# Attention layers of four batches in one sequence, with the projection row broadcast through DRAM

## The chip, the cores and the metric

The kernel runs on one core of one Trainium2 chip. The metric is the device time of one execution in microseconds (us). Three runs of the kernel before took 3220.69, 3226.43 and 3228.97 us; their median, 3226.43 us, is the time before.

## What is computed

Four layers of a graph network act on `x`, 16 batches of 1024 nodes with 256 features, all in float32. `adj` is a 1024 x 1024 matrix with few nonzero entries. Layers 0 and 1 make messages along the edges. Layers 2 and 3, which the change is about, are two attention layers of the same form:

```python
feats  = einsum('bni,oi->bno', data, W1)
f1     = einsum('bno,o->bn', feats, W2) + b2[0]
logits = f1[:, :, None] + f1[:, None, :]
coefs  = softmax(leaky_relu(logits) + adj, axis=-1)
vals   = einsum('bij,bjo->bio', coefs, feats)
out    = vals + bias2 + data
```

Each logit is a sum of a number of the row's node and a number of the column's node. So the kernel needs f1 twice: as a column, one number on each partition for each tile of 128 nodes, and as a row, the same 1024 numbers on every partition.

## The kernel before

The 16 batches are worked on in four groups of four (`GB = 4`). `z` holds a batch's features, feature-major, in two halves of 128 features. A tile of nodes has 128 of them, so a batch has `NT = 8` tiles; a half `v` of the nodes has `HN = 512`, which is `HT = 4` tiles.

A group has these stages. `with_edges` ends layer 0: it loads scores (`gd`, 512 KB each) and multiplies them with `hw` of all four batches. `layer_one` is layer 1, of two batches at a time: `projected`, and then `neighbours`, whose 16 steps load each 256 KB of the turned adjacency matrix (`adjT_in`, L1122, a ring of three buffers) and multiply. `pair_layers` holds the attention layers of the same two batches. In groups 0 to 2 a group is `with_edges`, `layer_one` of batches 0 and 1, their `pair_layers`, `layer_one` of batches 2 and 3, their `pair_layers`. The last group has work of its own beside it (`far_ahead`).

An attention layer of one batch is one `front` and two `sums`. `front` (L969) projects: eight tiles of two products each, 128x257 out, where column 257 is f1; ScalarE copies each tile from PSUM to `feats` (L980). Then come the `scales` (L988): eight TensorE transposes (L1002), each of a column of f1 stretched to 128 x 128 by an access pattern of step zero, so that its transpose is f1 as a row on all partitions; one more transpose (L1007) for the largest f1; VectorE's reduction of that (L1008); two ScalarE instructions that evict the rows with a Relu (L1011); exponentials (L1014 to L1016); eight scalings of `feats` (L1018). `sums` (L1027) makes for each of the eight tiles `jt` a weight tile `m` of 128 x 512 on VectorE (L1036, four buffers), multiplies it on TensorE into four PSUM banks, and hands the sums to `finish`. For layer 2 that is `second`, which divides by the totals (L1049, L1210) and transposes back (L1217, L1221); for layer 3 `third`, which adds the residual (L1241, L1247, L1251) and stores from ScalarE's queue (L1252).

Most TensorE products go through one helper, so their line is L126; they are told apart by the tiles that they read. One product has two records.

`scales` and the transposes back are not written where they are made but put on a list, `later`, which `catch_up` empties at the second tile of the next `front` or the first tile of the next `sums`. The order of a pair is written out by hand:

```python
                m0 = yield from front(z[0], gat2)
                m1 = yield from front(z[1], gat2)
                yield from sums(m0, 0, second(0))
                yield from sums(m0, 1, second(0))
                yield from sums(m1, 0, second(1))
                m0 = yield from front(z[0], gat3)
                yield from sums(m1, 1, second(1))
                yield from sums(m0, 0, third(0))
                m1 = yield from front(z[1], gat3)
                ahead()
```

and three more `sums`. `ahead` loads for the next group four `hw` (L892, 1024 KB each, from a pool of five buffers that `feats` and `y` use too) and four `z` (L900, 1024 KB each, into the four buffers of the present `z`).

Beside all this runs a side stream, the edge scores of the next groups. One step of it is a gather on GpSimd's queue (L695), two VectorE passes over 128 x 1024 (L805 and L807) and four ScalarE sums (L811), later a scatter (L700). `Side.along` writes such steps between the steps of the main work, 0.255 of a step per microsecond that a main step is said to take (the numbers in `yield`). `paced` makes the first pass of a step wait for a product six back, so that a side step does not run far ahead of the main work. The framework that writes the queues keeps near the order of the program text, but may put a later instruction first where an earlier one is not ready.

Of the kernel before, what the change touches and what calls it, by code (L numbers as in the profile page):

```python
# [9 lines left out]
F32 = mybir.dt.float32  # L10
# [55 lines left out]
def gnn_stack_kernel(  # L66
# [120 lines left out]
    class Attention:  # L187


        def __init__(self, W1, W2, b2, bias2, name):  # L190
            self.W1 = W1
            self.w2 = column(W2, f"{name}_w2")
            self.b2 = everywhere(b2, 1, f"{name}_b2")
            self.bias2 = column(bias2, f"{name}_bias2c")
            self.wT = const.tile([P, DH, D + 1], F32, name=f"{name}_wT")
            self.rows = const.tile([P, DH, P], F32, name=f"{name}_rows")

        def prepare(self, nat):
            transpose_weight(self.wT[:, :, :D], nat)
            ps = bank()  # L200
            for dh in range(DH):
                for oh in range(DH):
                    nc.tensor.matmul(
                        ps[:, dh : dh + 1], nat[:, oh, dh * P : (dh + 1) * P], self.w2[:, oh : oh + 1],
                        start=oh == 0, stop=oh == DH - 1,
                    )
            nc.vector.tensor_copy(self.wT[:, :, D], ps[:, :DH])
            for dh in range(DH):
                nc.vector.tensor_copy(self.rows[:, dh, :], self.wT[:, dh, D : D + 1].to_broadcast([P, P]))
# [26 lines left out]
    def prepare(t):  # L236
        transpose_weight(l1wT, t[:, 0])
        for i, gat in enumerate((gat2, gat3)):
            gat.prepare(t[:, 1 + i])
# [22 lines left out]
    part_d = dram.tile([XT * P + P, 2 * D], F32, name="part_d")  # L262

# [411 lines left out]
    with tc.If(listed > 0) as arm:  # L675
        with ExitStack() as stack:
# [292 lines left out]
            def front(x, weights):  # L969

                wT = weights.wT
                f = ttile("feats").rearrange("p (t d) -> p t d", t=NT)
                for jt in range(NT):
                    ps = bank()
                    for dh in range(DH):
                        product(
                            ps[:, : D + 1], x[:, dh, jt * P : (jt + 1) * P], wT[:, dh, :],
                            start=dh == 0, stop=dh == DH - 1,
                        )
                    nc.scalar.activation(f[:, jt, :], ps[:, : D + 1], AF.Copy)  # L980
                    if jt == 1:
                        catch_up()
                    yield 0.86
                made = {}
                later.append(lambda: scales(f, weights, made))
                return made

            def scales(f, weights, made):  # L988
# [4 lines left out]
                ta = small.tile([P, NT], F32, tag="tau", name="tau")  # L993
# [16 lines left out]
                for v in range(NV):  # L1010
                    nc.scalar.activation(r[:, v * HN : (v + 1) * HN], banks[v], AF.Relu, bias=sh[:, 3:4])  # L1011
                nc.vector.tensor_scalar(sh[:, 1:2], sh[:, 0:1], -0.01, None, ALU.mult)
# [8 lines left out]
            later = []  # L1021

            def catch_up():
                while later:
                    later.pop(0)()

            def sums(made, v, finish):  # L1027

                if "f" not in made:
                    catch_up()  # L1030
# [3 lines left out]
                for jt in range(NT):  # L1034
# [9 lines left out]
                    if jt == 0:  # L1044
                        catch_up()
# [71 lines left out]
            def neighbours(y, z, cols):  # L1117
                n = cols.stop - cols.start
                acc = [[bank() for _ in range(DH)] for _ in range(2)]
                for jt in range(NT):  # L1120
                    a = three.tile([P, HN], F32, tag="a", name="adjT_in")[:, :n]
                    nc.sync.dma_start(a, adjT_d[jt][:, cols])  # L1122
                    for i in range(2):
                        for eh in range(DH):
# [3 lines left out]
                            )  # L1128
                    yield 3.4 * n / HN
# [66 lines left out]
            def pair_layers(b, z, ahead, first):  # L1196


                yield from first


                def second(i):
                    def finish(v, acc, share):
                        cols = slice(v * HN, (v + 1) * HN)
                        vals = []
                        for c in range(HT):
                            if c % 2 == 0:
                                pair = four.tile([P, 2, D], F32, tag="st", name="val")
                            val = pair[:, c % 2, :]
                            nc.scalar.activation(val, acc[c][:, :D], AF.Identity, scale=share[:, c : c + 1])  # L1210
                            vals.append(val)

                        def turn_back():
                            ps = [bank() for _ in range(DH)]
                            for c in range(HT):
                                for dh in range(DH):
                                    nc.tensor.transpose(  # L1217
                                        ps[dh][:, c * P : (c + 1) * P], vals[c][:, dh * P : (dh + 1) * P], ident
                                    )
                            for dh in range(DH):  # L1220
                                nc.vector.scalar_tensor_tensor(  # L1221
                                    z[i][:, dh, cols], ps[dh], gat2.bias2[:, dh : dh + 1], z[i][:, dh, cols],
                                    ALU.add, ALU.add,
                                )
                        later.append(turn_back)
                    return finish


                def third(i):
                    def finish(v, acc, share):  # L1230
                        if v == 0:
                            for dh in range(DH):
                                nc.scalar.activation(
                                    z[i][:, dh, :], z[i][:, dh, :], AF.Identity, bias=gat3.bias2[:, dh : dh + 1]
                                )
                        for c in range(0, HT, 2):
                            ps = bank()
                            it = v * HT + c
                            for k in range(2):
                                for dh in range(DH):  # L1240
                                    nc.tensor.transpose(  # L1241
                                        ps[:, k * D + dh * P : k * D + (dh + 1) * P],
                                        z[i][:, dh, (it + k) * P : (it + k + 1) * P], ident,
                                    )
                            st = four.tile([P, 2, D], F32, tag="st", name="st")
                            for k in range(2):
                                nc.scalar.activation(  # L1247
                                    st[:, k, :], acc[c + k][:, :D], AF.Identity, scale=share[:, c + k : c + k + 1]
                                )
                            both = st.rearrange("p t d -> p (t d)")  # L1250
                            nc.vector.tensor_tensor(both, both, ps, ALU.add)  # L1251
                            nc.scalar.dma_start(  # L1252
                                out[b + i, it * P : (it + 2) * P].rearrange("(t p) d -> p t d", p=P), st
                            )
                    return finish


                m0 = yield from front(z[0], gat2)
                m1 = yield from front(z[1], gat2)
                yield from sums(m0, 0, second(0))  # L1260
                yield from sums(m0, 1, second(0))
                yield from sums(m1, 0, second(1))
                m0 = yield from front(z[0], gat3)
                yield from sums(m1, 1, second(1))
                yield from sums(m0, 0, third(0))
                m1 = yield from front(z[1], gat3)
                ahead()
                yield from sums(m0, 1, third(0))
                yield from sums(m1, 0, third(1))
                yield from sums(m1, 1, third(1))  # L1270
                assert not later

            def ahead(g):
                if g < NGR:
                    loaded.append(([load_hw(g * GB + i) for i in range(GB)], load_z(g)))
                    for load, i in z_loads:
                        load(i)
                    z_loads.clear()
# [22 lines left out]
            for g in range(NGR):  # L1301
# [4 lines left out]
                one = pair_layers(g * GB, z[:2], lambda: None, layer_one(z[:2]))  # L1306
                if g < NGR - 1:
                    side.along(one, RATE[1])
                    side.along(pair_layers(g * GB + 2, z[2:], lambda: ahead(g + 1), layer_one(z[2:])), RATE[1])
                else:  # L1310
                    for _ in far_ahead(z[2:], one):
                        pass
                    for _ in pair_layers(g * GB + 2, z[2:], lambda: None, from_lists(z[2:], msg)):
                        pass
# [3 lines left out]
    with arm.Else():  # L1318
        with ExitStack() as stack:
# [15 lines left out]
            prepare(load_naturals(stage))  # L1335
# [110 lines left out]
```

## Time and profile before

| What | Value |
|---|---|
| Median of three runs | 3226.43 us |
| The profiled execution's own time | 3225.44 us |
| Its span, first to last instruction | 3224.0 us |
| TensorE busy | 3128.0 us, 97% |
| VectorE busy | 2353.0 us, 73% |
| ScalarE busy | 1946.6 us, 60% |
| GpSimd busy | 1816.5 us, 56% |
| Mean granted TensorE clock | 0.99 |
| Moved by DMA | 687.48 MB, 213 GB/s |

The rows of the profile show one execution. PE is TensorE's matmuls, PEld its weight loads, DVE is VectorE, ACT is ScalarE, POOL is GpSimd and SP is SyncE; a `q` behind the name is the engine's queue of instructions, where DMAs are issued. In a group of instructions the numbers are the busy time, the mean duration of one in ns, and the idle time of the engine before them with what ended it. Durations of neighbouring instructions overlap, since they are pipelined: what one costs is the distance from start to start.

### The profile page before, as it was taken

To read this page: it belongs to the slowest core of one execution; us is meant where nothing else is said; L and a number is where in the kernel's file an instruction comes from. 1 tells how busy PE (TensorE), PEld (TensorE's weight loads), DVE (VectorE), ACT (ScalarE), POOL (GpSimd) and SP (SyncE) were. 2 spreads that over 40 slices of the span, in tenths; PEclk is the share of its full clock that TensorE was granted. 3 is DMA by queue.
4 is the path that set the end of the run, shared out by engine and by line. 5 is a ranking of instruction groups with operands and counts; after the bars stand their busy time and mean duration, and the time that the engine had idled before them with its cause. 6 is when DMAs were issued, how large, how long until landed. Compare 5 with 4: busy or idle time off the path is not lost. (4 is left out here: it accounts for less than half of the span.)

```text
span 3224.0 us, 39221 instructions
## 1 busy us (share of the span) xinstructions
PE 3128.0 (97%) x12122; PEld 2205.5 (68%) x12122; DVE 2353.0 (73%) x3174; ACT 1946.6 (60%) x6512; POOL 1816.5 (56%) x1483
## 2 busy tenths in 40 slices
PE   9899999999999999999999999899999999999899
PEld 5444545555457668678876867787687688858787
DVE  7797778677774689789768978877798891148744
ACT  3244555666668777567977757688676774414242
POOL 1146777676764666657566665556676651076600
PEclk9999999999999999999999999999999999999999
DMA  9888888888889765756876575587657644475600
GB/s 321 294 320 317 266 288 270 273 239 247 269 280 343 207 172 148 230 156 206 293 235 170 158 219 178 164 285 236 188 151 213 186 141 144 126 251 147 172 3 28
DMA packets 281898, 687.48 MB, mean 213 GB/s; under 512 B 45184, under 2 KB 137344, under 8 KB 274512
## 3 DMA queue, kind: packets, MB, share of 16 engines
q0 software_dynamic: 128224, 387.80, 41.3%
q1 hardware_dynamic: 126016, 245.98, 22.2%
q10 hardware_dynamic: 27440, 51.13, 4.2%
q8 instruction: 97, 1.59, 0.2%
q14 instruction: 121, 0.99, 0.1%
HBM read 553.45 MB, written 131.32 MB: 212 GB/s over the span
## 5 line engine op out<-in xcount | busy, mean ns | idle before, releaser
L811 ACT ACTIVATE z<-z 128x256 f32<-128x256 f32 x2432 | 979.5, 406 | 639.1 <-DVE z L807 580.9
L805 DVE TENSOR_TENSOR z<-z,u 128x1024 f32<-128x1024 f32 x608 | 738.7, 1220 | 437.0 <-PE bank L126 274.6
L126 PE MATMUL bank<-feats,m 128*128 128x257 f32 x4096 | 921.3, 383 | 19.3 <-DVE m L1036 17.8
L695 POOL DMA_INDIRECT z<-v_d,slot_v x512 | 637.2, 1244 | 479.9 <-ACT z L811 274.3
L126 PEld LDWEIGHTS bank<-feats,m 128*128 128x128 f32 x4096 | 770.6, 191 | 137.9 <-DVE m L1036 20.0
L700 POOL DMA_INDIRECT dense_d<-gt,slot_at x512 | 645.9, 1262 | 186.5 <-issue 140.1
L807 DVE SCALAR_TENSOR_TENSOR z<-z,w2r 128x1024 f32<-128x1024 f32 x608 | 737.9, 1220 | 9.0
L126 PE MATMUL bank<-gc,hw 128*128 128x256 f32 x2048 | 458.9, 386 | 25.2 <-ACT gc L1064 15.5
L811 ACT ACTIVATION_READ_ACCUMULATOR z<-z 128x1 f32 x2432 | 461.6, 190 | 0.0
L126 PEld LDWEIGHTS bank<-gc,hw 128*128 128x128 f32 x2048 | 390.6, 193 | 93.1 <-ACT gc L1064 24.0
L126 PE MATMUL bank<-adj_sb,h 128*128 128x512 f32 x1024 | 444.6, 594 | 4.5 <-ACT st L322 3.0
L1036 DVE SCALAR_TENSOR_TENSOR m<-rho,tau,adj_sb 128x512 f32<-128x512 f32 x512 | 375.3, 743 | 67.8 <-PE bank L126 62.1
L126 PE MATMUL bank<-adjT_in,y 128*128 128x512 f32 (+1 forms) x960 | 401.0, 579 | 2.0 <-DMA adjT_in<-adjT_d 1.4
L126 PEld LDWEIGHTS bank<-adj_sb,h 128*128 128x128 f32 x1024 | 194.9, 191 | 245.5 <-issue 239.8
L126 PE MATMUL bank<-w,hT 128*128 128x512 f32 (+1 forms) x1024 | 336.3, 489 | 0.0
L126 PEld LDWEIGHTS bank<-adjT_in,y 128*128 128x128 f32 x960 | 181.9, 190 | 216.8 <-issue 204.2
L1064 ACT ACTIVATE gc<-gd 128x1024 f32<-128x1024 f32 x128 | 264.7, 2071 | 95.3 <-PE bank L126 60.8
L126 PEld LDWEIGHTS bank<-w,hT 128*128 128x128 f32 x1024 | 195.7, 192 | 142.4 <-issue 122.9
L126 PE MATMUL bank<-g_wT,z 128*128 128x257 f32 x1024 | 234.0, 383 | 2.5 <-DVE z L1115 2.5
L695 POOL DMA_INDIRECT z<-v_d,x_node x96 | 122.2, 1273 | 176.2 <-ACT z L811 118.7
L126 PEld LDWEIGHTS bank<-g_wT,z 128*128 128x128 f32 x1024 | 193.2, 192 | 33.4 <-DVE z L1115 3.5
L695 POOL DMA_INDIRECT z<-y_d,slot_v x96 | 108.3, 1128 | 56.6 <-DVE msg L1174 41.0
(161 smaller groups left out, 2370.2 us busy)
## 6 DMA issues: line engine op xcount, KB each, us to landing
gd<-dense_d SPq DMA_DIRECT2D x128, 512.0 KB
dense_d<-zero ACTq DMA_DIRECT2D x64, 512.0 KB
adjT_in<-adjT_d SPq DMA_DIRECT2D x112, 256.0 KB
h<-in_x_dram SPq DMA_DIRECT2D x19, 1024.0 KB
u_d<-st SPq DMA_DIRECT2D x64, 256.0 KB
v_d<-st SPq DMA_DIRECT2D x64, 256.0 KB
hw_d<-st SPq DMA_DIRECT2D x64, 256.0 KB
u<-u_d POOLq DMA_DIRECT2D x32, 512.0 KB
```

The lines of the kernel that those rows point to most:

```text
L126: recent.append(nc.tensor.matmul(*args, **kw))
L695: return nc.gpsimd.indirect_dma_start(out=dst, out_offset=None, in_=src[:], in_offset=bass.IndirectOffsetOnAxis(ap=at, axis=0), **how,)
L700: return nc.gpsimd.indirect_dma_start(out=dst[:], out_offset=bass.IndirectOffsetOnAxis(ap=at, axis=0), in_=src, in_offset=None,)
L805: paced(nc.vector.tensor_tensor(z, z, u, ALU.add))
L807: nc.vector.scalar_tensor_tensor(zk, zk, 0.0, w2r[:, None, :].to_broadcast([P, GB, D]), ALU.max, ALU.mult)
L811: nc.scalar.activation(zk[:, c, :], zk[:, c, :], AF.Copy, accum_out=s[:, k, c : c + 1])
L1036: nc.vector.scalar_tensor_tensor(m, r[:, cols], ta[:, jt : jt + 1], ea[:, jt, cols], ALU.max, ALU.mult)
L1064: paced(nc.scalar.activation(gc, gd.rearrange("p n i -> p i n"), AF.Copy), 16)
```

## The change

In groups 0 to 2 the two `pair_layers` become one `group_layers`: `layer_one` of batches 0 and 1, the projection of batch 0, `layer_one` of batches 2 and 3, and then a sequence over eight pairs (layer, batch), in which the projection of the next pair is written before the sums of the present one. The loads for the next group are written at the last two of the eight. `scales` is kept for the last group. In the others `to_row` and `from_row` take its place: VectorE gathers f1 as a 128 x 9 tile (eight columns and the maximum of each partition), TensorE transposes it once, ScalarE copies the 9 x 128 result, SyncE stores it to a row in DRAM and loads that row back to all 128 partitions (512 KB, and 64 KB for the maxima). Three ticks later VectorE reduces the maxima and one ScalarE Relu of 128 x 1024 works on the loaded row. `later` now holds counts, and `tick`, called at every second tile of `sums`, every fourth of `front` and every step of `neighbours`, counts them down. The list `rows` that a fallback branch uses is moved into that branch.

```diff
+            def tick():
+                for what in later:
+                    what[0] -= 1
+                while later and later[0][0] <= 0:
+                    later.pop(0)[1]()
...
-            def front(x, weights):
+            def front(x, weights, row=None):
...
-                    if jt == 1:
-                        catch_up()
+                    if jt % 4 == 1:
+                        tick()
                     yield 0.86
                 made = {}
-                later.append(lambda: scales(f, weights, made))
+                if row is None:
+                    later.append([1, lambda: scales(f, weights, made)])
+                else:
+                    later.append([1, lambda: to_row(f, weights, made, row)])
                 return made
+
+            def to_row(f, weights, made, row):
+
+                r = two.tile([P, N], F32, tag="rho", name="rho")
+                tops = two.tile([P, P], F32, tag="tops", name="tops")
+                column = small.tile([P, NT + 1], F32, tag="column", name="column")
+                nc.vector.tensor_copy(column[:, :NT], f[:, :, D])
+                nc.vector.tensor_reduce(column[:, NT:], f[:, :, D], AX.X, ALU.max)
+                ps = bank()
+                nc.tensor.transpose(ps[: NT + 1, :P], column, ident)
+                nc.scalar.activation(r[: NT + 1, :P], ps[: NT + 1, :P], AF.Copy)
+                nc.sync.dma_start(row.rearrange("(t p) -> t p", p=P), r[: NT + 1, :P])
+                nc.sync.dma_start(r, bcast_rows(row[:N], N))
+                nc.sync.dma_start(tops, bcast_rows(row[N:], P))
+                later.append([3, lambda: from_row(f, weights, made, r, tops)])
+
+            def from_row(f, weights, made, r, tops):
+                sh = small.tile([P, 4], F32, tag="shift", name="shift")
+                nc.vector.tensor_reduce(sh[:, 0:1], tops, AX.X, ALU.max)
+                nc.vector.scalar_tensor_tensor(sh[:, 3:4], weights.b2, 2.0, sh[:, 0:1], ALU.mult, ALU.add)
+                nc.scalar.activation(r, r, AF.Relu, bias=sh[:, 3:4])
+                scaled(f, made, r, sh)
...
             def sums(made, v, finish):
 
-                if "f" not in made:
-                    catch_up()
+                while "f" not in made:
+                    tick()
...
-                    if jt == 0:
-                        catch_up()
+                    if jt % 2 == 0:
+                        tick()
                     yield 1.7
...
+            def group_layers(g, z):
...
+                def fronts(layer, i):
+                    gat = (gat2, gat3)[layer]
+                    made[layer, i] = yield from front(z[i], gat, row_d[layer, g * GB + i])
...
+                yield from layer_one(z[:2])
+                yield from fronts(0, 0)
+                yield from layer_one(z[2:])
+                order = [(layer, i) for layer in range(2) for i in range(GB)]
+                for n, it in enumerate(order):
+                    if n + 1 < len(order):
+                        yield from fronts(*order[n + 1])
+                    if n == 2 * GB - 2:
+                        hw = [load_hw((g + 1) * GB + i) for i in range(GB - 1)]
+                        nz = load_z(g + 1)
+                    if n == 2 * GB - 1:
+                        hw.append(load_hw((g + 1) * GB + GB - 1))
+                        loaded.append((hw, nz))
+                    for _ in range((0, 2, 1)[max(0, n - 2 * GB + 3)]):
+                        load, i = z_loads.pop(0)
+                        load(i)
+                    yield from both_halves(*it)
...
-                one = pair_layers(g * GB, z[:2], lambda: None, layer_one(z[:2]))
                 if g < NGR - 1:
-                    side.along(one, RATE[1])
-                    side.along(pair_layers(g * GB + 2, z[2:], lambda: ahead(g + 1), layer_one(z[2:])), RATE[1])
+                    side.along(group_layers(g, z), RATE[1])
```

`scaled` is the rest of `scales` from L1012 on, unchanged; `both_halves` is the two `sums` of one pair with their `finish`; `second` and `third` take `z` as an argument and put the transposes back on `later` with a count of 1.

## The prediction, made before the changed kernel was run

> **What bounds the kernel now.** I read the page first, then windows cut at the stages, then the chain of waits and the timelines of one pair of batches.
>
> ```profile
> PE 3128.0 (97%) x12122; PEld 2205.5 (68%) x12122; DVE 2353.0 (73%) x3174; ACT 1946.6 (60%) x6512; POOL 1816.5 (56%) x1483
> ```
>
> TensorE has work 97% of the span, so whatever leaves TensorE can shorten the kernel, unless another engine is full in that stage. The windows tell (PE, PEld, DVE, ACT, POOL busy; granted clock; DMA share; GB/s): two pairs of attention layers and the layer one between the first and the second.
>
> ```profile
> 1156.00:1311.00 155.00, 152.04 (x740) 130.59 (x739) 144.61 (x216) 113.20 (x421) 102.93 (x77) 1.00 0.56 158
> 1311.00:1380.00 69.00, 69.00 (x196) 36.77 (x195) 48.42 (x49) 40.97 (x166) 44.61 (x36) 1.00 0.73 221
> 1726.00:1881.00 155.00, 152.01 (x736) 129.27 (x735) 145.51 (x216) 114.07 (x422) 104.32 (x81) 1.00 0.57 161
> ```
>
> In the attention stage VectorE is busy 145 of 155 us, in layer one only 48 of 69. The 73% of the page is a mean over both. The clock is 1.00: nothing is lost there. Next, pieces of the chain (start, length):
>
> ```profile
> 2968.61 0.87 PE bank L1002 x8
> 2969.48 0.11 PE bank L1007
> 2969.59 13.88 PE bank L126 x64
> ```
>
> Eight stretched transposes hold TensorE 0.87 us, one 0.11 us, and half of a batch's sums (64 records) 13.88 us, 0.217 us a record. A pair of batches is then 4 projections of 32 records (27.8), 8 halves (111.0), 4 x 0.98 of row transposes and 8 x 0.87 of other transposes (7.0): 149.7 us, against 155 measured. The waits of TensorE over the three groups:
>
> ```profile
> PE bank L126 <- DVE m L1036: 17.8, 9, 8.1
> PE bank L126 <- issue: 4.5, 4, 2.5
> ```
>
> VectorE's weight tile `m` is what TensorE waits for. Two of the nine are 11.4 us together, and there VectorE itself sat for a gather of the side stream:
>
> ```profile
> 2046.41 1.23 DVE L805 TENSOR_TENSOR z<-z,u 128x1024 f32<-128x1024 f32 x1 [8.19 <-DMA z<-v_d,slot_v]
> ```
>
> The remaining 6.4 us are the change's to win; one is the start of a pair, where the scaled `feats` come late:
>
> ```profile
> 1173.17 2.84 PE L126 MATMUL bank<-feats,m 128*128 128x257 f32 x12 [1.99 <-DVE m L1036]
> ```
>
> **The change part by part.** Times are set against the profiled execution, 3225.4 us (span 3224.0), which lies 1.0 us below the median.
>
> *Row transposes.* Groups 0 to 2 have 24 projections. Each loses eight transposes, 0.87 us; the ninth stays as the transpose of the column. 24 x 0.87 = 20.9 us off TensorE.
>
> *Order.* With a projection one whole batch ahead, its scaled `feats` are ready some 28 us before the sums want them. Of the 6.4 us, plus about 3 us of short waits for ScalarE's evictions, I take 3 us back; bounds 0 and 9.5. Runs of three halves without a projection between them, in which VectorE falls behind, become runs of two, which speaks for it.
>
> *VectorE's room.* It is busy 144.4 us in a pair (mean of the first five). After the change TensorE wants 149.7 - 4 x 0.87 = 146.2 us, so VectorE would be at 99% of it, and with only four `m` buffers two engines that nearly balance wait for each other. Of the 20.9 us I give 6 back (1 us a pair); bounds 0 and the whole 20.9. VectorE's own instructions hardly change: a copy of 128x8 more, about 0.16 us like the reduction at L995, 24 x 0.16 = 3.8 us of its time, 0.4 us of it on the path.
>
> *The detour through DRAM.* The trace shows no small store followed by its load, so I bound it. For the load, a 512 KB score load from the same queue:
>
> ```profile
> 2678.17 1.27 SPq L886 DMA_DIRECT2D gd<-dense_d  x3
> 2682.18 3.92 ACT L1064 ACTIVATE gc<-gd 128x1024 f32<-128x1024 f32 x2 [16.53 <-DMA gd<-dense_d]
> ```
>
> From issue to use is 4.0 us. The upper end is a 256 KB load under gathers:
>
> ```profile
> 2475.39 53.02 SPq L1122 DMA_DIRECT2D adjT_in<-adjT_d  x16
> 2510.63 17.43 PE L126 MATMUL bank<-adjT_in,y 128*128 128x512 f32 x40 [0.93 <-DMA adjT_in<-adjT_d]
> ```
>
> The step that waits is the twelfth, its load the ninth of this row (three were issued ahead), so issued near 2475.39 + 8 x 3.43 = 2502.9: 7.7 us. The store has no near row; the last output store, issued until 3218.6, and the end of the span at 3224.0 bound it by 5.4 us, and below by 0. I take 3. With the copy on VectorE (0.16), the transpose (0.27) and ScalarE's copy (0.3, plus 0 to 2.4 behind the four sums of a side step, so 1.5 in all), the chain is 0.2 + 0.3 + 1.5 + 3 + 4 = 9 us; ends 4.7 and 16.
>
> `from_row` stands six steps of the sums after `to_row`: 6 x 8 x 0.217 = 10.4 us, of which VectorE may be one step (1.7) ahead. The chain thus has 8.7 us, and misses it by 0.3 us in the mean. What is queued behind the reduction is the next `m`, for which TensorE waits; one `m` made ahead covers 1.7 us of a miss. I put +3 us over 21 projections, since some rows come later than the mean; ends 0 and, at 16 us, 21 x (7.3 - 1.7) = 118 us, which would need every row to meet a crowded queue.
>
> The Trainium skill, "DMA: Bandwidth & Descriptors" (section Anatomy of one DMA — SWDGE (gpsimd) path), gives about 2.0 us fixed for a DMA plus its bytes at 436 GB/s; by it the store is an estimated 2.0 and the load 3.4, the chain 7.4 us, and the term 0 rather than 3. The same page (section Latency and other measured facts) speaks against the change: HBM access is 0.2 us on average but 2 us at high load, and two dependent transfers pay it twice; no row here shows it. Left to the rows above, the sum stays as it is.
>
> *SyncE's queue.* The broadcast load waits for the store and holds what stands behind it. Only the projection of batch 0 has time-critical loads there: `adjT_in` of the second layer one. Queues here do not follow the text strictly:
>
> ```profile
> 1281.01 30.68 SPq L900 DMA_DIRECT2D z<-zb_d  x2
> ```
>
> Two loads of the next group's `z` stand in the first pair, though they are written in the second. And the row of 16 `adjT_in` loads above begins at 2475.39, after TensorE had begun that stage at 2471.8: three were issued far ahead, 3 x 3.43 = 10.3 us of work. They cover the 9 us. I take 0; without that cover the first load would come behind store and broadcast, 3 + 4 + 2 us, three times: 27 us. The moved `hw` and `z` loads wait for buffers as before, and the last `hw` gets its buffer two halves (28 us) before its use: 0, or at twice the 4.0 us of a load of half the size, 3 x 8 = 24 us uncovered. Their transfers can delay a row behind them; that is in the upper end of the detour.
>
> *ScalarE and the rest.* Two evictions (0.63 apart) become one Relu of 128x1024 (1.05, like L1014) and a small copy: even, and ScalarE is busy 113 of 155. 24 x 0.58 MB more on 687 MB, with DMA at 57% in this stage: 0. The four copies of `rows` leave the start: 4 x 0.22 us of VectorE under TensorE's work, 0. The last group keeps its form.
>
> Sum: -20.9 - 3 + 6 + 0.4 + 3 = -14.5, so 3225.4 - 14.5 = 3210.9, rounded 3211 us.
>
> **The rivals.** *The DRAM row is late (slower).* One mechanism: VectorE's reduction of the maxima, in its place before the next `m`, waits for the load, 21 times. The gain without the detour is 17.5 us, or 0.83 us for each; with the 1.7 covered, the change loses from a miss of 2.5 us, a chain of 11.2 us. At a chain of 12.6 us it is 21 x 2.2 = 46 us less 17.5: 3254 us. For it: VectorE has no room to catch up, and gathers share the DMA engines. Against it: 9 us by the nearest rows.
>
> *VectorE is the bound (no change).* The 0.87 us go into longer waits for `m`: -3 and +3, +0.4, so 3225.8 us, say 3225. For it: 99%. Against it: VectorE itself waits in a pair, and part of that room goes with the better order:
>
> ```profile
> DVE z L805 <- PE bank L126: 7.4, 11, 1.9
> ```
>
> *All of it comes (faster).* No detour, no balance loss, all short waits gone: 3225.4 - 20.9 - 9.5 = 3195 us. It needs VectorE to keep up at 99%.
>
> *The change doesn't do what it says:* the framework could write the projections elsewhere than a batch ahead; the DRAM path is then used all the same, and the time falls among the cases above.
>
> **How the numbers follow.** About 0.3% (9.7 us) is what a measurement of this kernel can tell from no change: its runs spread 8.3 us. Forecast 0.43 (its own range 3200 to 3222, of which 0.06 lies within 0.3%), late row 0.25, VectorE the bound 0.17, all of it 0.15. Faster: 0.37 + 0.15 = 0.52. Same: 0.06 + 0.17 = 0.23. Slower: 0.25. The range leaves out the better half of the last case and the worse part of the late row: 3192 to 3254.
>
> **What would show it.** Right: L1002 at 64 records instead of 256, pairs of about 151 us, TensorE's wait for `m` outside the two gather waits under 6 us, no VectorE wait for `tops` over 1 us. Wrong: VectorE idle before the reduction of `tops` by several us in most projections; `m` waits of 20 us or more in all; or TensorE waiting for `adjT_in` at the start of the second layer one.

## The result and the profile after

| | before | after |
|---|---|---|
| Median of four runs, us | 3224.97 (3220.69 to 3228.97) | 3255.68 (3243.81 to 3264.21) |
| Ratio after to before, 95% interval | | 1.009 (1.0068 to 1.0111) |
| Profiled execution: own time, span, us | 3225.44, 3224.0 | 3247.9, 3246.2 |
| Mean granted TensorE clock | 0.99 | 0.986 |

The changed kernel is slower by 0.9%, some 29 us, where 0.45% faster was forecast. The first line of the page's engine table shows that the work did leave TensorE:

```profile
PE 3123.0 (96%) x11930; PEld 2192.1 (68%) x11930; DVE 2353.0 (72%) x3194; ACT 1949.6 (60%) x6512; POOL 1829.9 (56%) x1483
```

TensorE has 192 records fewer, which is 24 projections times eight, and yet only 5.0 us less busy time. In the groups by line the stretched transposes (L1002, now L1044) are left in the last group only, and the transpose of the column takes their place (L1017):

```profile
L1044 PE MATMUL bank<-ident,feats 128*128 128x128 f32 x64 | 9.2, 276 | 0.8 <-ACT feats L998 0.8
L1017 PE MATMUL bank<-ident,column 128*9 128x128 f32 x24 | 6.5, 271 | 1.0 <-DVE column L1015 0.9
```

The windows of the three sequences, each from about the end of the second `layer_one` to the end of the sums (columns as before: PE, PEld, DVE, ACT, POOL busy; granted clock; DMA share; GB/s):

```profile
1221.00:1544.00 323.00, 299.76 (x1385) 253.23 (x1384) 283.43 (x426) 219.52 (x803) 200.65 (x150) 0.97 0.60 180
1808.00:2123.00 315.00, 295.23 (x1383) 248.74 (x1382) 284.14 (x430) 218.66 (x799) 204.53 (x153) 0.99 0.62 185
2392.00:2708.00 316.00, 297.52 (x1384) 251.56 (x1382) 269.16 (x415) 206.12 (x753) 195.59 (x142) 0.98 0.54 165
```

They last 318.0 us in the mean. The forecast's count gives two pairs without the projection that stands before: 2 x 146.2 - 6.9 = 285.5 us. So 32.5 us of each are lost. Before, two pairs lost 2 x (155 - 149.7) = 10.6 us by the two windows that the forecast went by; all six pairs took 941 us, which is 14.3 us lost for two. VectorE is less busy than before (279 of 318 us in the mean, against 283 of 314 for two pairs of the six): it does not lack time over the whole sequence, it waits. TensorE's waits over the three groups:

```profile
PE bank L126 <- DVE m L1076: 29.6, 17, 9.4
PE bank L126 <- ACT st L1283: 10.8, 12, 2.5
...
PE bank L1253 <- ACT val L1246: 6.2, 7, 1.6
PE bank L126 <- DVE st L1287: 5.3, 1, 5.3
PE bank L126 <- DVE share L1089: 4.4, 2, 2.2
PE bank L126 <- DMA adjT_in<-adjT_d: 2.3, 1, 2.3
```

The wait for `m` went from 17.8 us to 29.6 us. Waits for evictions were 5 us before (L1247, L1210, L980); they and the waits for VectorE's part in them (`st`, `share`) are now 26.7 us, the other rows above without the load. The waits of SyncE's queue have one row that the waits of before do not list, and those of VectorE two:

```profile
SPq L1020 <- DMA row_d<-rho: 42.4, 18, 6.6
...
DVE shift L1026 <- DMA tops<-row_d: 33.5, 17, 4.5
DVE st L1287 <- ACT st L1283: 27.9, 8, 8.0
```

The first and second are the detour: the load waits for the store, and VectorE's reduction of the maxima waits for the load, 17 times. The third is something else: VectorE's residual addition waits for ScalarE's evictions, up to 8 us at a time. One such place, at the boundary between the two halves of a batch's sums, from the timelines of the three engines (start, length, instruction, idle before it). VectorE:

```profile
1489.36 0.29 DVE L1026 TENSOR_REDUCE shift<-tops 128x1 f32<-128x128 f32 x1 [1.52 <-DMA tops<-row_d]
1489.56 0.74 DVE L1076 SCALAR_TENSOR_TENSOR m<-rho,tau,adj_sb 128x512 f32<-128x512 f32 x1
...
1498.58 0.69 DVE L1287 TENSOR_TENSOR st<-st,bank 128x512 f32<-128x512 f32 x1 [4.23 <-ACT st L1283]
```

ScalarE:

```profile
1490.46 1.15 ACT L1028 ACTIVATE rho<-rho,shift 128x1024 f32<-128x1024 f32 x1 [0.88 <-ACT z L817]
...
1491.71 1.04 ACT L1060 ACTIVATE rho<-rho 128x1024 f32<-128x1024 f32 x1
...
1493.35 3.29 ACT L1064 ACTIVATE feats<-feats 128x256 f32<-128x256 f32 x8
...
1497.73 1.53 ACT L1283 ACTIVATE st<-bank,share 128x256 f32<-128x256 f32 x4
```

TensorE:

```profile
1493.75 2.00 PE L126 MATMUL bank<-feats,m 128*128 128x257 f32 x8 [2.25 <-DVE share L1089]
1498.24 5.42 PE L126 MATMUL bank<-feats,m 128*128 128x257 f32 x16 [2.49 <-ACT st L1283]
```

The reduction waits 1.52 us with the next `m` behind it. It also releases ScalarE's burst: the Relu, the exponentials, eight scalings, with the four sums of one side step between them. From 1490.46 to 1497.73 no eviction runs. But the first half's sums are complete just then, and the evictions (L1283) that free its banks stand behind the burst. TensorE stops for 2.49 us, VectorE's addition 4.23 us, and the next `m` with it. Before, most bursts began on the second to fifth tile of a half and were over before its end. After, all but the first of each group straddle the boundary or follow it at once: they begin between the last two tiles of the first half and the first of the second, and their scalings begin on the first two tiles of the second half or just before it.

### The profile page after: what moved, and what is told of

Same layout as the page of the kernel before. It is cut to its first block, busy times and chain, and to the rows that moved or that the text cites. A ratio compares the mean times of both kernels' runs of the same rounds, so it can differ in the third digit from the quotient of the medians.

```text
span 3246.2 us, 38932 instructions
## 1 busy us (share of the span) xinstructions
PE 3123.0 (96%) x11930; PEld 2192.1 (68%) x11930; DVE 2353.0 (72%) x3194; ACT 1949.6 (60%) x6512; POOL 1829.9 (56%) x1483
## 4 chain that ended last, share of the span: by engine, by line
PE 39%; DVE 5%; ACT 5%; DMA 4%; issue 3%; POOL 1%; SPq 0%; ACTq 0%; DVEq 0%; POOLq 0%
PE bank L126 38%; DVE z L811 2%; DMA tops<-row_d 2%; ACT z L817 2%; DVE z L813 1%; DVE m L1076 1%; ACT feats L1064 1%; DMA row_d<-rho 1%; PE bank L1253 1%; POOL z L701 1%; DMA z<-v_d,slot_v 1%; DMA adjT_in<-adjT_d 1%; ACT gc L1104 0%; ACT rho L1060 0%; ACT rho L1028 0%
## 5 line engine op out<-in xcount | busy, mean ns | idle before, releaser
L126 PE MATMUL bank<-feats,m 128*128 128x257 f32 x4096 | 931.3, 386 | 49.1 <-DVE m L1076 29.6
L701 POOL DMA_INDIRECT z<-v_d,slot_v x512 | 644.5, 1259 | 473.6 <-ACT z L817 260.8
L813 DVE SCALAR_TENSOR_TENSOR z<-z,w2r 128x1024 f32<-128x1024 f32 x608 | 737.4, 1219 | 8.5
L126 PEld LDWEIGHTS bank<-gc,hw 128*128 128x128 f32 x2048 | 392.8, 194 | 93.7 <-ACT gc L1104 27.7
```

The source lines that it names most:

```text
L126: recent.append(nc.tensor.matmul(*args, **kw))
L701: return nc.gpsimd.indirect_dma_start(out=dst, out_offset=None, in_=src[:], in_offset=bass.IndirectOffsetOnAxis(ap=at, axis=0), **how,)
L813: nc.vector.scalar_tensor_tensor(zk, zk, 0.0, w2r[:, None, :].to_broadcast([P, GB, D]), ALU.max, ALU.mult)
```

## The experiments

Four theories. **A:** the wait for the DRAM row. **B:** the place of ScalarE's burst, at the half boundary, ahead of the evictions. **C:** the order of the projections by itself. **AB:** A and B together. Times are ratios to the kernel before, run beside each kernel on the same chip. From the single profiled execution of each comes "layers": the time of the three groups from the last product with scores to the first of the next group (layer one and attention). It runs from the start of that last product. Its "loss" is what remains above TensorE's products and transposes at their own pace (437.0 us a group with eight stretched transposes, 430.1 us without, 431.8 us in few_turns). The last column is VectorE's waits for the maxima, in brackets where they are loaded from `x`.

| Kernel | Ratio (95%) | Span | Layers | Loss | `tops` waits |
|---|---|---|---|---|---|
| before | 1 | 3224.0 | 1359.8 | 48.8 | none |
| after | 1.0090 (1.0068 to 1.0111) | 3246.2 | 1390.7 | 100.5 | 33.5 |
| after_again | 1.0094 (1.0068 to 1.0120) | 3238.0 | 1384.8 | 94.7 | 32.5 |
| order_only | 1.0008 (0.9993 to 1.0023) | 3224.5 | 1363.8 | 52.9 | none |
| order_at6 | 1.0067 (1.0041 to 1.0093) | 3252.2 | 1384.0 | 73.0 | none |
| few_turns | 0.9933 (0.9911 to 0.9955) | 3199.4 | 1347.9 | 52.5 | none |
| const_row | 1.0092 (1.0071 to 1.0112) | 3248.2 | 1379.4 | 89.3 | (9.4) |
| late5_const | 1.0078 (1.0050 to 1.0107) | 3244.1 | 1377.8 | 87.5 | (9.5) |
| const_pin3 | 0.9973 (0.9957 to 0.9989) | 3218.6 | 1362.0 | 71.8 | none |
| const_pin5 | 0.9985 (0.9972 to 0.9998) | 3225.1 | 1357.5 | 67.4 | none |
| split | 1.0089 (1.0064 to 1.0113) | 3242.2 | 1390.9 | 100.6 | 38.2 |
| reduce3_burst5 | 1.0052 (1.0033 to 1.0071) | 3246.4 | 1383.8 | 93.7 | 36.3 |
| early2 | 1.0086 (1.0069 to 1.0104) | 3256.7 | 1400.0 | 109.7 | 39.5 |
| late5 | 0.9987 (0.9972 to 1.0002) | 3212.3 | 1354.6 | 64.4 | 12.9 |
| late6 | 1.0038 (1.0024 to 1.0052) | 3246.1 | 1375.5 | 85.3 | 12.5 |
| now6 | 1.0112 (1.0081 to 1.0143) | 3272.9 | 1406.8 | 116.5 | 2.9 |
| tops_first3 | 1.0062 (1.0045 to 1.0079) | 3249.0 | 1392.1 | 101.8 | 33.1 |
| tops_first5 | 1.0017 (1.0001 to 1.0032) | 3228.5 | 1363.7 | 73.5 | 14.9 |

**after_again**: the changed kernel once more.

> The changed kernel once more, beside the three below on the same chip, as their measure. Both theories: 0.5 to 1.2% above the kernel before.

The ratio repeats. The layers differ by 6 us between two executions of one kernel, so single traces are read to no better than that.

**order_only**: the new order with the old `scales`.

```diff
-                    made[layer, i] = yield from front(z[i], gat, row_d[layer, g * GB + i])
+                    made[layer, i] = yield from front(z[i], gat)
```

> The new order of four batches with the old transposes of the row. Theory A (the row's way through DRAM costs the time: VectorE's reduction waited 33.5 us for it in 17 places): with the detour gone the kernel is at or below the kernel before, 3210 to 3228 us, and the waits for m return below 20 us. Theory B (the place of ScalarE's burst: Relu, exponentials and eight scalings, 7 us, stand at the end of a half, where the sums want to be evicted): also at or below, since here the burst stands at the start of a half; the evictions' wait (VectorE's add waiting for ScalarE, 27.9 us) is gone. Theory C (the order itself, eight pairs with no layer one between them, leaves VectorE no room): 3240 us or more, as the changed kernel.

The order alone neither gains nor costs by the times; the layers show +4.0 us, less than two executions differ by. C, as a cost of 29 us, is out.

**few_turns**: the kernel before with six of the eight stretched transposes left out.

```diff
-                    for c in range(HT):
-                        ...
+                    nc.tensor.transpose(ps[:, :P], f[:, v * HT, D : D + 1].to_broadcast([P, P]), ident)
```

> The kernel before with two row transposes a projection instead of eight; the row then repeats its first 128 nodes in each half, so part of the computation is left out. TensorE loses 6 x 0.108 us in each of 32 projections, 20.8 us. If TensorE's time is the bound, 0.5 to 0.65% faster. If VectorE's lack of room takes it back, under 0.3% faster. It measures the term that the prediction put at 20.9 less 6.

32 projections lose 6 x 0.108 us each, 20.8 us. The kernel gains 0.67%, 21.6 us (14.5 to 28.7): all of it. In the layers of the three groups it is 11.9 of 15.6 us. So in the order of before, time taken off TensorE comes through, and VectorE does not eat it.

**order_at6**: no DRAM; the old `scales` at the seventh tile, the place of `from_row`.

```diff
-                    later.append([1, lambda: to_row(f, weights, made, row)])
+                    later.append([4, lambda: scales(f, weights, made)])
```

> The new order with the old transposes and no way through DRAM, but scales is run four ticks after the projection instead of one: at the seventh tile of a half, where from_row stands in the changed kernel. Theory A (the wait for the row): no row, so as with the scales at the first tile, within 0.3% of the kernel before. Theory B (ScalarE's burst collides with the evictions at the end of a half): slower than the kernel before by 0.5 to 1%, with evictions waiting for ScalarE by 15 us or more, though nothing goes through DRAM.

Against order_only only the place differs, and it costs 0.59%, some 19 us; 20.2 us in the layers. The wait of VectorE for evictions, which order_only does not show, is there without any DRAM row:

```profile
DVE st L1287 <- ACT st L1283: 33.3, 6, 7.8
```

One of the six, ScalarE first and then VectorE:

```profile
1504.07 1.25 ACT L1053 ACTIVATE rho<-bank,shift 128x512 f32<-128x512 f32 x2
...
1506.94 3.29 ACT L1064 ACTIVATE feats<-feats 128x256 f32<-128x256 f32 x8
...
1510.93 1.54 ACT L1283 ACTIVATE st<-bank,share 128x256 f32<-128x256 f32 x4
```

```profile
1511.78 0.69 DVE L1287 TENSOR_TENSOR st<-st,bank 128x512 f32<-128x512 f32 x1 [7.05 <-ACT st L1283]
```

That is B without A. But more has moved than ScalarE's burst: the transposes of `scales` and the PSUM banks that they fill stand at the boundary too, and the changed kernel has one small transpose there. So the 20 us are not the price of the burst alone.

**const_row** and **late5_const**: the row is loaded from `x`, and the load waits for no store, which is made from a tile of its own; at three and at five ticks.

```diff
-                nc.sync.dma_start(r, bcast_rows(row[:N], N))
-                nc.sync.dma_start(tops, bcast_rows(row[N:], P))
+                nc.sync.dma_start(r, bcast_rows(x0[0], N))
+                nc.sync.dma_start(tops, bcast_rows(x0[1], P))
```

> The row and the maxima are loaded from rows of x, which are there from the start, so that nothing waits for the store; the projection's own row is left out of the result, though it is still turned and stored. All else, and the place of from_row, as in the changed kernel. A: the wait for the maxima is gone (under 3 us) and the time falls by 20 to 35 us. B: the wait for the maxima is gone, but the evictions' wait stays near 28 us, and the time falls by less than 12 us. C: no gain.

> Five ticks, and the row loaded from x, so that nothing waits for a store; the projection's own row is left out of the result. Beside the five ticks with the row's own store it tells what the way through DRAM still costs there. A: a further 0.3 to 0.6% faster than five ticks alone. B: no difference over 0.3%, unless the framework writes the burst to another place.

Neither got faster, and neither tells A from B. With nothing to wait for, the framework wrote reduction and burst earlier, into the first to fifth tile of the first half, in both kernels alike. (The waits in brackets are over at 1011 us, before the layers.) There the burst meets the evictions that prepare the transposes back. This row of TensorE's waits in const_row was 6.2 us in the changed kernel:

```profile
PE bank L1256 <- ACT val L1249: 22.4, 14, 4.2
```

**const_pin3**: const_row, with the reduction tied to a product six back by `paced`, so that it stays where it stands in the changed kernel.

```diff
-                nc.vector.tensor_reduce(sh[:, 0:1], tops, AX.X, ALU.max)
+                paced(nc.vector.tensor_reduce(sh[:, 0:1], tops, AX.X, ALU.max))
```

> The row from x again (nothing waits for a store; the projection's own row is left out of the result), but VectorE's reduction is tied to the sixth product back, so that the framework can't write it and ScalarE's burst earlier than in the changed kernel. Theory AB (two costs: the wait for the row, some 27 us, and the burst's place, some 20 us): the wait for the maxima is gone, the place stays, 0 to 0.3% above the kernel before (-20.7 + 20 + 4). Theory B alone (the place is all): 0.8 to 1.1% above, as the changed kernel. Theory A alone: 0.4% or more below.

Now the scalings begin 0 to 1.5 tiles into the second half, and once just before it (0 to 2.0 in the changed kernel), and the row is always there. VectorE's wait for evictions stays; the wait for `tops` is gone, and that for `m` falls from 29.6 to 13.4 us:

```profile
DVE st L1290 <- ACT st L1286: 24.1, 7, 7.9
...
PE bank L126 <- DVE m L1079: 13.4, 12, 2.2
```

The kernel is 1.2% faster than the changed one. In the layers it is 26 us (1387.7, the mean of the changed kernel's two, less 1362.0), in the spans 23.5 us. The ratios say 38 us, but they come from different sessions and chips, in which the kernel before itself took 3213.25 and 3236.47 us. All three show A; the layers, which repeat to 6 us, give it some 26 us. The ratio, 0.27% below the kernel before, lies between what was expected of A and B together and of A alone.

**const_pin5**: the same at five ticks.

> The row from x (the projection's own is left out of the result), the reduction tied to the sixth product back, five ticks: neither wait nor bad place. Both causes gone, so what the change says it does is left: -20.7 us of transposes and +4 us of order, 0.4 to 0.6% below the kernel before. If a third cost is left, 0.3% or less below.

The scalings now begin at 3.5 to 5.6 tiles of the second half, free of both costs, and the kernel is no faster than const_pin3; the loss is 4.4 us smaller, not 20. The 0.15% below the kernel before is what was expected if a third cost is left. Part of what went was replaced: 8.6 us once for copies of a projection behind ScalarE's other work (L1002), 6.8 us once behind a side step on VectorE (L813). So the price of B in the changed kernel isn't the 20 us of order_at6.

**split**: the eight scalings two ticks later than the rest; **reduce3_burst5**: the whole burst two ticks later than the reduction.

```diff
                 for jt in range(NT):
                     nc.scalar.activation(f[:, jt, :D], ...)
# split: these eight in a function of their own, later.append([2, scalings])
# reduce3_burst5: Relu, exponentials and these eight in one, later.append([2, lambda: burst(f, made, r, sh)]);
#   the Relu is tied to a product six back by paced
```

> The changed kernel with the eight scalings (3.3 us of the burst) put two ticks later, into the second half; the Relu and the exponentials stay where they are, and so does the wait for the row. A: the wait for the maxima stays near 33 us and the time stays 0.7 to 1.2% above the kernel before. B: at least half of the loss goes, to 0 to 0.5% above.

> The changed kernel with VectorE's reduction where it is (three ticks, so it waits for the row as before) and ScalarE's Relu, exponentials and scalings two ticks later. AB: the wait for the maxima stays near 33 us, the evictions' waits go, 0.2 to 0.5% above the kernel before. B alone: as five ticks for both, within 0.3% of the kernel before. A alone: as the changed kernel, 0.8% or more above.

split gains nothing, though VectorE's wait for evictions falls to 13.5 us: the waits for `tops` (38.2 us) and `m` (29.9 us) stay. reduce3_burst5 gains 0.4% on the changed kernel with 36.3 us of `tops` waits left. Moving B away while A stays is worth 12 us by the ratios and 4 us in the layers.

Four of the kernels differ in A and B and in little else. Their layers, in us:

| | burst at the boundary | burst mostly within the second half |
|---|---|---|
| the row is waited for | 1387.7 (the changed kernel, mean of two) | 1383.8 (reduce3_burst5) |
| the row is there | 1362.0 (const_pin3) | 1357.5 (const_pin5) |

A is worth 26 us in either column and B 4 us in either row, so neither changes the other. For B that is less than the 6 us by which two executions of one kernel differ.

**early2**: two ticks instead of three.

> from_row two ticks after to_row, at the fifth tile of the half: the row has 3.5 us less. If nothing covers the wait, VectorE's wait grows from 33 us to 70 to 100 us, and the time to 1.5 to 3% above the kernel before, less what the burst gains by its place in the middle of a half (up to 0.6%). If 1.7 us of each are covered, 0.5 to 1.2% above.

Same time, so the edit missed what it was to change: from the column's copy to the reduction the trace has 9.8 us in the mean against 9.7. The framework put the reduction nearly where three ticks had put it.

**late5** and **late6**: five and six ticks, and `tick` runs every entry that is due, not the head alone (so it does in now6, split, reduce3_burst5, late5_const, const_pin5 and tops_first5).

```diff
-                while later and later[0][0] <= 0:
-                    later.pop(0)[1]()
+                due = [what for what in later if what[0] <= 0]
+                later[:] = [what for what in later if what[0] > 0]
+                for what in due:
+                    what[1]()
...
-                later.append([3, lambda: from_row(f, weights, made, r, tops)])
+                later.append([5, lambda: from_row(f, weights, made, r, tops)])
```

> from_row five ticks after to_row instead of three, so that the row has 17 us instead of 10 and ScalarE's burst falls into the middle of the second half. A: the wait for the maxima falls from 33.5 us to under 5, 3205 to 3225 us. B: the evictions' wait falls from 27.9 us to under 8, also 3205 to 3225 us. C: no gain, 3240 us or more.

> from_row six ticks after to_row. AB: the wait for the maxima under 5 us (12.9 with five), the burst at the fifth to seventh tile of the second half, still before its evictions: 0.1 to 0.5% faster than the kernel before. B: no better than five ticks, since the burst nears the next evictions.

late5 takes back the whole of the 0.9% and ends level with the kernel before; its waits for the row are

```profile
DVE shift L1028 <- DMA tops<-row_d: 12.9, 7, 3.5
```

and most bursts are clear of the boundary. late6 loses 0.5% again with the same waits for the row (12.5 us): at six ticks most scalings, from the sixth to eighth tile on, end with the half and meet the evictions before the next transposes back, 22.3 us of waits of L1255 for `val` against 7.9 us in late5. The place of the burst is a cost by itself here too.

**now6**: `to_row` at once behind the projection, `from_row` six ticks later.

> to_row at once behind the projection, from_row six ticks on: its place is that of five ticks, the row has one step more. AB: the wait for the maxima under 5 us, 0.2 to 0.6% faster than the kernel before, unless TensorE waits for the column in front of the sums (under 10 us in all).

The slowest of all, by a cost that was expected to stay under 10 us: TensorE's transpose of the column now stands directly behind the last product of the projection, and TensorE waits for ScalarE's and VectorE's copies.

```profile
PE bank L1019 <- DVE column L1017: 47.6, 20, 11.5
```

**tops_first3** and **tops_first5**: the 64 KB of maxima are loaded ahead of the 512 KB row, at three and at five ticks.

```diff
-                nc.sync.dma_start(r, bcast_rows(row[:N], N))
-                nc.sync.dma_start(tops, bcast_rows(row[N:], P))
+                nc.sync.dma_start(tops, bcast_rows(row[N:], P))
+                nc.sync.dma_start(r, bcast_rows(row[:N], N))
```

> The changed kernel with the 64 KB of maxima loaded before the 512 KB row, so that VectorE's reduction waits for the small load alone and ScalarE's Relu for the large one. If VectorE's wait is what costs: it falls from 33 us to under 15 and the time to 0.3 to 0.7% above the kernel before. If the wait only moves to ScalarE: still 0.8% or more above.

> The same with five ticks: VectorE's wait falls from 12.9 us to under 6, and the time is 0.2 to 0.5% below the kernel before, if each microsecond of that wait costs about one; if the rest of the wait is covered, as with five ticks alone, 0.0 to 0.25% below.

Without the first projection of each group, the maxima are used 8.9 us after the column's copy instead of 9.7, so their load did come forward. But VectorE was also free for the reduction a microsecond earlier, 7.5 us after the copy instead of 8.5, and the waits are as long as before (33.1 us). So tops_first3 doesn't settle what a shorter wait is worth. One kernel is 0.3% below the version with the other order, one 0.3% above it. The order of the two loads doesn't matter by more than small shifts of place do.

No version that computes the whole is clearly faster than the kernel before: late5 is the best, and its interval reaches 1.0002.

## Why the prediction was wrong, by its own steps

**Row transposes, -20.9: right as work that leaves TensorE.** The products and transposes of the three groups are 20.7 us shorter, and few_turns shows that such time comes through in the order of before.

**VectorE's room, +6: too much in the old order, too little in the new.** few_turns gave back 0 by the times and 3.7 us in the layers. In the new order, const_pin5 has neither the wait nor the burst at the boundary, and its layers are only 6.3 us shorter than those of order_only (1357.5 against 1363.8): 14.4 of the 20.7 us did not come through. VectorE was busy for 278 of the 307 us of a sequence there, so it did have idle time; but no run tells how much of the 14.4 us is the balance of the two engines, and the rival "VectorE is the bound" is only refuted for the old order.

**Order, -3: wrong sign, small.** +2.6 us (-2.3 to +7.4) by the times, +4.0 in the layers.

**Detour, +3: the step that failed.** The chain was well sized: 9.7 us in the mean of 21 projections from the column's copy to the reduction, against 9, with the store's part (from its issue to the load's) 2.7 us against 3, and 1.3 to 7.2. The estimate from the Trainium skill, "DMA: Bandwidth & Descriptors" (Anatomy of one DMA — SWDGE (gpsimd) path), 7.4 us and no cost, was farther off; that section is about DMAs issued from GpSimd, and these were issued from SyncE. What failed is "one `m` made ahead covers 1.7 us of a miss". VectorE waited 1.2 us in the mean at the 21 places, 25.7 us together, and const_pin3, without these waits, is 26 us shorter in the layers. As near as single executions can tell, nothing was covered. With four `m` buffers and VectorE at 99% the forecast's own figures spoke against a reserve there. The rival "The DRAM row is late" was the right mechanism; it was given 21 x 2.2 = 46 us from a chain of 12.6, while a miss of 1.2 us was enough because the 1.7 us did not exist.

**ScalarE "even", 0: right in the busy time, incomplete in the place.** The busy times are even (1949.6 against 1946.6 us). But the burst was costed by how long it is and not by what stands behind it on its engine. Where the old `scales` are put at the boundary it costs 20 us (order_at6), transposes and banks included; in the changed kernel the burst itself is worth 4 us by the four kernels above. With A and B both gone, const_pin5 still loses 19 us more than the kernel before, and late5, where both are nearly gone, 16 us. In const_pin5 that is the 4 us of the order and the 14 us of transposes that did not come through, in waits with many releasers. What sets these is open. The shift of where the framework puts things, and gather waits of VectorE that range from 13 to 31 us over these executions, hide effects under some 0.3%.

**SyncE's queue, 0: right.** TensorE waited for `adjT_in` once, 2.3 us, against 0.9 before; in the first group, three loads of the second `layer_one` were issued at 1138.9 to 1145.8, ahead of the row's store at 1170.9.

**Sum.** -20.7 for the transposes, +14.4 of them that did not come through, +4 for the order, +26 for the row and +4 for the burst's place give +28; the layers show +30.9 and +25.0, the times +29. The terms are differences along one chain of kernels, so that they add up proves nothing. They say that the wait for the row is the largest part, and that half as much has no shown cause.

**What would show it.** L1002 (now L1044) at 64 records came true. The signs of "wrong" came true as well: VectorE idle ahead of the reduction in 17 of 24 projections, though by 2.0 us in the mean and not by several, and waits for `m` of 29.6 us. No sign watched ScalarE's evictions.

## What to carry to other kernels

Here waits of 1.2 us in the mean were paid in full, as near as the layers tell, on an engine whose work fills 279 of the 285.5 us that TensorE needs for its stage: before a transfer is put in front of its next instruction, ask how far ahead it really is, in instructions made and not yet used. An instruction that is moved brings with it what it releases: look at which evictions stand behind a released burst, at the new place and not in the mean, since a burst of 7 us ahead of a bank's eviction stopped TensorE and VectorE both here. To separate a wait from a place, take the wait away and tie the instruction where it was; without the tie the order is rewritten and the run answers another question.

## What the runs showed of the hardware

Short idles of TensorE cost more than their length, because the granted clock falls. After a gather wait of 9.37 us in the changed kernel:

```profile
1400.00:1404.00 4.00, 0.00 (x0) 0.00 (x0) 0.00 (x0) 0.00 (x0) 3.08 (x4) 0.96 0.34 74
1404.00:1408.00 4.00, 0.00 (x0) 0.00 (x0) 2.65 (x7) 1.28 (x3) 3.09 (x4) 0.50 0.94 335
...
1410.00:1412.00 2.00, 2.00 (x6) 1.54 (x6) 2.00 (x3) 2.00 (x7) 0.00 (x0) 0.50 0.96 375
1412.00:1414.00 2.00, 2.00 (x6) 1.18 (x4) 0.42 (x1) 2.00 (x10) 0.00 (x0) 0.52 0.25 94
1414.00:1416.00 2.00, 1.70 (x8) 1.42 (x8) 1.10 (x2) 1.93 (x8) 0.94 (x1) 1.00 0.19 25
```

```profile
1408.68 5.43 PE L126 MATMUL bank<-feats,m 128*128 128x257 f32 x12 [9.37 <-DVE m L1076]
```

Twelve records take 5.43 us, where they take 12 x 0.217 = 2.6 at full clock. By the trace's record of the granted clock, of which the rows show the means, it fell at 1403.66, 4.4 us into the idle time, which began at 1399.3, and came back at 1413.90, 5.2 us after work resumed. At the half boundary above it fell at 1499.24, a microsecond after work had resumed, and for 3.41 us; the 16 records there take 5.42 us instead of 3.5:

```profile
1498.00:1500.00 2.00, 1.76 (x6) 1.49 (x7) 1.42 (x2) 1.27 (x4) 1.60 (x2) 0.81 0.87 239
1500.00:1502.00 2.00, 2.00 (x6) 1.60 (x5) 2.00 (x3) 0.00 (x0) 1.26 (x1) 0.50 0.75 172
1502.00:1504.00 2.00, 2.00 (x11) 1.66 (x11) 2.00 (x4) 1.71 (x8) 0.00 (x0) 0.84 0.90 313
```

The Trainium skill, "TensorE: Matmul & The Clock Gate" (Part 1: The HAM clock gate), says half rate after an idle window of about 3.4 us, full rate after about 3.4 us of sustained work, and that the window runs freely. These traces agree with the window: the first half-rate stretch lasted 10.24 us, three times 3.41, and the two falls are 95.6 us apart, 28 times that. They differ in what an idle window is. In the 3.41 us before the fall at 1499.24 TensorE worked 1.0 us. From the first layer one to the last attention layer of the three groups, the clock fell 129 times in the 18 traces of this case, always on such a grid, each time after a window in which TensorE was busy between 0 and 53%; no window under 43% kept the full clock. In 79 of the 129 no single idle time in the window reached 3 us. So two kernels with equal idle time can differ in how it falls into the windows.

The loss beyond TensorE's listed idle times in the layers was 25.7 us before and 41.4 us after: of the 51.7 us more that the layers lost, 15.7 came behind the waits and not in them. Products at half clock are 10.7 us of that (16.3 us lost against 5.6; 10.1 in after_again).
